# One transformer block on one core: two exponentials as powers on GpSimd, two stores issued later, a new order of the last steps, and where VectorE's transposes begin

## The chip, the core and the metric

The kernel runs on one core of one Trainium2 chip. Time is device time in microseconds (us), the median of several executions. A profile is one further execution, taken by the hardware profiler; its span runs from the first to the last instruction, and its own time is a little longer than the span.

The engines are named as in the profile: PE is TensorE's matmul stream, PEld its weight loads, DVE is VectorE, ACT is ScalarE, POOL is GpSimd and SP is SyncE, which issues most of the DMAs. A name such as L743 is line 743 of the kernel that was profiled; since the change adds lines, the same statement stands some lines lower in the changed kernel.

## The reference

The input `x` is 64 sequences of 32 tokens (2048 tokens) with 256 features. Three residual steps follow one another, each on a layer-normed `x`:

- cross attention with 16 heads to a context of 257 rows per sequence,
- self attention inside each sequence with 4 heads and rotary positions,
- a mixture of 8 experts, each token going to its two best ones.

The last is what the change touches. In short:

```python
scores = x @ Wr.T + br                       # 8 scores per token
w = softmax(scores)
idx = top_k(scores + biases_N, 2)            # two experts per token
val = w[idx] / w[idx].sum()                  # their weights
h = x @ Wl1[e] + bl1[e]; a, b = h[:512], h[512:]
y = (silu(a) * b) @ Wl2[e] + bl2[e]          # per expert e
out = x + sum over the two experts of val * y
```

## The kernel before

Tokens are worked in 16 tiles of 128 (`t` = 0 to 15). For each tile and each of its four sequences (`b`) a main loop emits the cross attention of that sequence. Between its matmuls it places pieces of other work: `near` is the rest of the tile just finished (output projection, self attention, routing), `far` the rest of the tile before that, `ahead` the queries of later tiles. The tuple `steps` says which of these is advanced at each of six places of a sequence, so it sets PE's order.

PE and SP run in the order in which the program is written. VectorE, ScalarE and GpSimd are ordered by a scheduler, so a change in the text can move instructions on them that it does not name. Each engine executes in order: an instruction that waits holds up all those behind it.

`route(t, xr)` transposes the normed tile, forms the 8 scores, finds the two best experts, forms the weights (the exponential on ScalarE at L509, then a mask, a sum, a reciprocal and a product on VectorE), counts places by a matmul (`pk`), and writes each row to its two slots of `routed` in DRAM by two indirect DMAs on GpSimd (L533). The last tiles, 14 and 15, are routed in the tail, beside expert blocks, whose Silu needs another table on ScalarE than the exponential.

The residual `x` of each tile is stored into `out` (L472) at the end of `self_attention`: from SP for tiles 0 to 13, from GpSimd's queue for 14 and 15. The experts' results are added onto `out` by scatters with an adding DMA (L743), also on GpSimd's queue.

The experts' work is cut into blocks of 128 rows of one expert. Six `early` blocks use only rows that the first tiles have routed and run beside the tail of tiles 14 and 15. When all is counted, `late_blocks` computes on VectorE a table of which expert, which rows and which weights each `late` block uses; 28 late blocks follow. A block is: `gathered` (SP loads its rows from `routed`), `prepared` (transpose to features by rows), `first_half` and `second_half` (16 matmuls each, `pa` and `pb`, with Silu on ScalarE and a product on VectorE), `combined` (8 matmuls `py`, bias, weight, scatter). Three pairs of buffers, the lanes, hold weights; block b uses lane (b + 2) % 3. A lane's weights, 1028 KB and 640 KB, are loaded only when the lane's next block has another expert, by `weights`, after the block three before has released them.

There are two ways to transpose a block. With `b < quarters`, the rows come as one DMA of 132.5 KB, PE transposes them (`pxT`, L670) and ScalarE copies the result from PSUM. Otherwise the rows come as four DMAs of 32 KB in runs of 64 floats and one of 4.5 KB, and VectorE transposes 32x32 pieces (L675). Early blocks use the first way, late ones the first for b < 3.

SP's DMAs take eight completion semaphores in turn; a DMA waits until the one eight places before it has landed. `gathered` of late block b is issued three blocks ahead. In the function `run`, for late block 0 it was issued after `last_early`, which closes the last early block and loads the weights of late block 2.

The string given to `do` writes out the tail: `near` and `far` are steps of tiles 15 and 14, `xN`, `aN`, `bN`, `cN` are prepared, first half, second half and combined of early block N.

Of the kernel before, what the change touches and what calls it, by code (L numbers as in the profile page):

```python
# [9 lines left out]
FP = mybir.dt.float32  # L10
U32 = mybir.dt.uint32
AF = mybir.ActivationFunctionType
# [4 lines left out]
P = 128  # L17
# [12 lines left out]
NE = 8  # L30
# [20 lines left out]
def block_kernel(  # L51
# [33 lines left out]
    make_identity(nc, ident)  # L85
    minus_half = const.tile([P, 1], FP, name="minus_half")
    nc.gpsimd.memset(minus_half, -0.5)
    zero = const.tile([P, 1], FP, name="zero")
    nc.gpsimd.memset(zero, 0.0)
    expert_id = const.tile([P, NE], FP, name="expert_id")  # L90
# [295 lines left out]
    def self_attention(t, xn):  # L386
# [80 lines left out]
        for k in range(2):  # L467
            nc.tensor.matmul(po, oT[:, k, :], awo_sb[:, k, :], start=(k == 0), stop=(k == 1))  # L468
        nc.vector.tensor_tensor(xs[t], po, xb, ALU.add)

        queue = nc.sync if t < NT - 2 else nc.gpsimd
        queue.dma_start(out=out[t * P : (t + 1) * P, :], in_=xs[t])  # L472

    def route(t, xr):

        nc.gpsimd.tensor_copy(xr[:, RW - 1 : RW], token[:, t : t + 1])
        xT = wk.tile([P, 2, P], FP, tag="xrT", name=f"xrT{t}")
        transposed(xT, xr, 2, f"r{t}", t < NT - 2)
        yield
        pr = bank([NE], f"pr{t}")  # L480
        for k in range(2):
            nc.tensor.matmul(pr, xT[:, k, :], wr_sb[:, k, :], start=(k == 0), stop=(k == 1))
        sc = sm.tile([P, NE], FP, tag="rsc", name=f"rsc{t}")
        nc.vector.tensor_tensor(sc, pr, br_bc, ALU.add)
        sel = sm.tile([P, NE], FP, tag="rsel", name=f"rsel{t}")
        nc.vector.tensor_tensor(sel, sc, bn_bc, ALU.add)
        top = sm.tile([P, 8], FP, tag="rtop", name=f"rtop{t}")
        nc.vector.max(top, sel)
        idx = sm.tile([P, 8], U32, tag="ridx", name=f"ridx{t}")
        nc.vector.max_index(idx, top, sel)  # L490
        idf = sm.tile([P, 2, 1], FP, tag="ridf", name=f"ridf{t}")
        nc.vector.tensor_copy(idf[:, :, 0], idx[:, 0:2])

        two = sm.tile([P, 2, NE], FP, tag="rtwo", name=f"rtwo{t}")
        nc.vector.tensor_tensor(
            two, expert_id2, idf.to_broadcast([P, 2, NE]), ALU.is_equal
        )
        both = sm.tile([P, NE], FP, tag="rboth", name=f"rboth{t}")
        nc.vector.tensor_tensor(both, two[:, 0, :], two[:, 1, :], ALU.add)
        boths[t] = both  # L500
        if t < NT - 2:


            fed = sm.tile([P, NE], FP, tag="rfed", name=f"rfed{t}")
            nc.vector.scalar_tensor_tensor(fed, both, not_last, carried[t], ALU.mult, ALU.add)
        nmx = sm.tile([P, 1], FP, tag="rnmx", name=f"rnmx{t}")
        nc.vector.tensor_reduce(nmx, sc, AX.X, ALU.max, negate=True)
        ex = sm.tile([P, NE], FP, tag="rex", name=f"rex{t}")
        nc.scalar.activation(ex, sc, AF.Exp, bias=nmx)  # L509
        nc.vector.tensor_tensor(ex, ex, both, ALU.mult)  # L510
        tot = sm.tile([P, 1], FP, tag="rtot", name=f"rtot{t}")
        nc.vector.tensor_reduce(tot, ex, AX.X, ALU.add)
        inv = sm.tile([P, 1], FP, tag="rinv", name=f"rinv{t}")
        nc.vector.reciprocal(inv, tot)
        ew = xr[:, D : D + NE]
        nc.vector.tensor_scalar(ew, ex, inv, None, ALU.mult)
        yield

        pk = bank([NE], f"pk{t}")
        if t < NT - 2:  # L520
            nc.tensor.matmul(pk, before_all, fed, start=True, stop=True)
        else:
            nc.tensor.matmul(pk, before, both, start=True, stop=False)
            nc.tensor.matmul(pk, of_last, seen[t - 1], start=False, stop=True)
        at = sm.tile([P, 1, NE], FP, tag="rat", name=f"rat{t}")
        nc.vector.tensor_tensor(at[:, 0, :], pk, region[:, 0, :], ALU.add)
        nc.vector.tensor_tensor(two, two, at.to_broadcast([P, 2, NE]), ALU.mult)
        slot = sm.tile([P, 2], FP, tag="rslot", name=f"rslot{t}")
        nc.vector.tensor_reduce(slot, two, AX.X, ALU.add)
        slots = sm.tile([P, 2], U32, tag="rslots", name=f"rslots{t}")  # L530
        nc.vector.tensor_copy(slots, slot)
        for k in range(2):
            nc.gpsimd.indirect_dma_start(  # L533
                out=routed[:, :],
                out_offset=bass.IndirectOffsetOnAxis(ap=slots[:, k : k + 1], axis=0),
                in_=xr,
                in_offset=None,
            )
        if t < NT - 1:
            seen[t] = sm.tile([P, NE], FP, tag="seen", name=f"seen{t}")  # L540
            nc.vector.tensor_tensor(seen[t], pk, both, ALU.add)  # L541
            carry(t)
# [236 lines left out]

    def late_blocks(done):  # L780

        bl = Blocks("late", LATE, lambda b: (b + 2) % LANES, 3)
        count = counted("late", NT - 2, NT - 1)
        nb = in_blocks(count, P - 1, "late")
        nc.vector.tensor_tensor(nb, nb, done, ALU.subtract)
# [65 lines left out]
    def rotary_tables():  # L851
# [78 lines left out]
        ("ahead", "far", "ahead", "near", "far", "ahead"),  # L930
        ("", "", "near", "near", "", "far"),
    )
    kvs, probs = {0: context0}, {}
    seqs = [(t, b) for t in range(NT) for b in range(4)]
    work = {"near": last_rows(), "far": iter(()), "ahead": cross_queries(0)}
# [88 lines left out]
    for n, (t, b) in enumerate(seqs):  # L1024
# [12 lines left out]
        if b == 0:  # L1037
# [4 lines left out]
            if t % 2 == 0 and t + 4 < NT:  # L1042
                for j in (t + 4, t + 5):
                    load_tokens(j)
        place = iter(steps[4 * (t % 2) + b])

        def step():
            name = next(place)
# [50 lines left out]
    def do(units):  # L1099
        for unit in units.split():  # L1100
            if unit in work:
                next(work[unit], None)
            else:
                b = int(unit[1:])
                {
                    "x": blocks.prepared,
                    "a": blocks.first_half,
                    "b": blocks.second_half,
                    "c": blocks.combined,
                }[unit[0]](b)  # L1110
                if unit[0] == "c" and b + 2 < EARLY:
                    blocks.weights(b + 2, (0, 1))

    do("near far x0")
    blocks.gathered(EARLY - 1)
    do("far near near a0 far x1 b0 near far near near c0 near a1 near far b1 x2 far a2 near c1")
    do("far near x3 b2 a3 near c2 near x4 b3 near a4")
    late, total = late_blocks(done)
    do("c3")
    for b in range(3):  # L1120
# [8 lines left out]

    def run(lo, hi, before=None):  # L1130
        for b in range(lo, hi):
            if b + 3 < hi and not (before and b == lo):
                blocks.gathered(b + 3)
            if b + 1 < hi:
                blocks.prepared(b + 1)
            blocks.first_half(b)
            if b > lo:
                blocks.combined(b - 1)
                if b - 1 + LANES < hi:
                    blocks.weights(b - 1 + LANES, (1,))  # L1140
            elif before:
                before()
                blocks.gathered(b + 3)
            blocks.second_half(b)
            if b + LANES < hi:
                blocks.weights(b + LANES, (0,))
            if b == 4:
                yield
        blocks.combined(hi - 1)
# [85 lines left out]
```

## Time and profile before

| | |
|---|---|
| median of 5 runs | 806.33 us (802.53 to 808.06) |
| the profiled execution | 807.24 us, span 805.5 us |
| PE busy | 770.8 us, 96% of the span |
| VectorE busy | 503.9 us, 63% |
| ScalarE busy | 368.9 us, 46% |
| GpSimd busy | 148.5 us, 18% |
| mean clock granted to TensorE | 0.994 |

The span has three stretches. Up to some 575 us the main loop keeps PE busy. From there to 638 us the tail of tiles 14 and 15 runs beside the six early blocks. Then come the late blocks: block 0 starts at 638.59 us; from block 6 on, at 676.03 us, they follow at 5.30 us each with no gap until 791 us; a last scatter ends the program.

In a timeline line, the columns are start, duration, engine, source line, operation, result and inputs, shape, and in brackets the idle time of the engine just before with what ended it. Where several instructions are merged, the duration is that of the group.

### The profile page before, as it was taken

The page shows a single profiled execution, that of the slowest core. Times are in us where ns is not written, and L with a number is a line of the kernel's source. Part 1 is how long each engine was busy: PE and PEld are TensorE (multiplying, and loading weights), DVE is VectorE, ACT ScalarE, POOL GpSimd, SP SyncE. Part 2 cuts the span into 40 slices and gives each one's busy share as a digit, 9 for nine tenths or more (in the row PEclk, how much of TensorE's full clock was granted, in tenths as well). Part 3 has the DMA queues.
Part 4 walks back from the last instruction along what each step waited for, and adds up shares of the span by engine and source line. Part 5 has one row for each costly group of instructions (what it writes and reads, how often), then busy time and mean ns, then how long its engine had stood idle before and what let it go on. Part 6 is the DMA issues. An engine that isn't in the chain of part 4 may idle for free.

```text
span 805.5 us, 15343 instructions
## 1 busy us (share of the span) xinstructions
PE 770.8 (96%) x5136; PEld 603.5 (75%) x5136; DVE 503.9 (63%) x2087; ACT 368.9 (46%) x1053; POOL 148.5 (18%) x211
## 2 busy tenths in 40 slices
PE   8899999999999999999999999999998989999994
PEld 7576777677767777777767777666688878999994
DVE  4657666766685677668577766768655633444442
ACT  3564556556465454546555555555426312122220
POOL 3001011120211111021111111121133312332332
PEclk9999999999999999999999999999999999999998
DMA  8540202021120202022020202110531597449432
GB/s 304 145 112 2 66 11 68 11 90 46 32 80 11 68 10 80 10 76 73 19 66 12 66 11 67 29 58 15 186 141 34 144 298 206 60 86 264 58 48 27
DMA packets 47138, 64.17 MB, mean 80 GB/s; under 512 B 22928, under 2 KB 38032, under 8 KB 45520
## 3 DMA queue, kind: packets, MB, share of 16 engines
q1 hardware_dynamic: 40528, 54.08, 21.5%
q0 software_dynamic: 6528, 9.06, 6.5%
q8 instruction: 43, 0.70, 0.4%
q14 instruction: 39, 0.32, 0.1%
HBM read 87.54 MB, written 13.16 MB: 125 GB/s over the span
## 4 chain that ended last, share of the span: by engine, by line
PE 79%; DVE 4%; DMA 3%; ACT 2%; issue 1%; POOL 1%; SPq 1%; POOLq 0%; ACTq 0%; DVEq 0%
PE pa L346 13%; PE s L313 12%; PE tp L336 7%; PE po L379 6%; PE pa_late L703 6%; PE pqh L289 5%; PE pb_late L703 5%; PE py_late L736 5%; PE pqkv L394 5%; PE pov L362 4%; PE pq L268 3%; PE apo L468 1%; ACT ov L370 1%; DMA lane<-in_wall 1%; PE pot L454 1%; DMA lane2a<-in_wall 1%
## 5 line engine op out<-in xcount | busy, mean ns | idle before, releaser
L318 ACT ACTIVATE pr<-s,nmx 128x257 f32<-128x257 f32 x256 | 122.2, 481 | 111.9 <-DVE nmx L317 100.4
L317 DVE TENSOR_REDUCE nmx<-s 128x1 f32<-128x257 f32 x256 | 105.5, 420 | 70.8 <-PE s L313 70.2
L313 PE MATMUL s<-kv,q 128*128 128x257 f32 x512 | 142.4, 387 | 1.9 <-ACT pr L318 1.4
L346 PE MATMUL pa<-pt,kv 128*128 128x512 f32 x256 | 123.3, 604 | 5.1 <-ACT ov L370 5.1
L313 PEld LDWEIGHTS s<-kv,q 128*128 128x128 f32 x512 | 89.2, 192 | 16.4 <-issue 2.7
L336 PEld LDWEIGHTS tp<-ident,pr 128*128 128x128 f32 x512 | 61.8, 144 | 30.8 <-issue 15.7
L325 DVE TENSOR_SCALAR pr<-pr,inv 128x256 f32<-128x256 f32 x256 | 80.2, 356 | 3.3
L336 PE MATMUL tp<-ident,pr 128*128 128x128 f32 x512 | 80.5, 279 | 1.6 <-DVE pr L325 1.6
L349 ACT COPY cT<-pa 128x512 f32<-128x512 f32 x64 | 37.5, 587 | 92.3 <-PE pa L346 92.3
L340 ACT COPY pt<-tp 128x512 f32<-128x512 f32 x128 | 75.5, 591 | 4.2 <-PE tp L336 3.2
L346 PEld LDWEIGHTS pa<-pt,kv 128*128 128x128 f32 x256 | 46.1, 190 | 39.6 <-issue 26.4
L743 POOL DMA_INDIRECT out_x<-y_late,to_late x28 | 43.5, 1555 | 109.8 <-DMA out_x<-y_late,to_late 41.8
L289 PE MATMUL pqh<-xqT,xwq_sb 128*128 128x256 f32 x256 | 60.8, 381 | 0.8 <-ACT xqT L196 0.8
L379 PE MATMUL po<-xwo_sb,ov 128*128 128x256 f32 x256 | 60.3, 379 | 0.0
L719 ACT ACTIVATE sa_late<-pa_late,lane 128x128 f32<-128x128 f32 x72 | 20.6, 368 | 75.0 <-PE pa_late L703 75.0
L379 PEld LDWEIGHTS po<-xwo_sb,ov 128*128 128x128 f32 x256 | 48.6, 190 | 6.6
L289 PEld LDWEIGHTS pqh<-xqT,xwq_sb 128*128 128x128 f32 x256 | 47.3, 190 | 7.9 <-ACT xqT L196 1.5
L318 ACT ACTIVATION_READ_ACCUMULATOR pr<-s,nmx 128x1 f32 x256 | 52.0, 203 | 0.0
L323 DVE RECIPROCAL inv<-sums 128x2 f32<-128x2 f32 x128 | 20.8, 162 | 46.2 <-ACT pr L318 45.5
L546 POOL TENSOR_SCALAR carried<-seen,is_last 128x8 f32<-128x8 f32 x15 | 5.3, 354 | 218.7 <-DVE seen L541 218.7
L533 POOL DMA_INDIRECT routed<-xr,rslots x32 | 33.2, 1039 | 59.6 <-DMA routed<-xr,rslots 18.3
L394 PE MATMUL pqkv<-awqkv_sb,xaT 128*128 128x512 f32 (+1 forms) x128 | 43.9, 486 | 0.0
(273 smaller groups left out, 1266.5 us busy)
## 6 DMA issues: line engine op xcount, KB each, us to landing
lane<-in_wall SPq DMA_DIRECT2D x24, 1028.0 KB
lane<-in_wall SPq DMA_DIRECT2D x24, 640.0 KB
lane2a<-in_wall SPq DMA_DIRECT2D x10, 1028.0 KB
kv<-in_ctx_t SPq DMA_DIRECT2D x16, 514.0 KB
kv<-in_ctx_a SPq DMA_DIRECT2D x16, 512.0 KB
lane2b<-in_wall SPq DMA_DIRECT2D x10, 640.0 KB
xg_late<-routed SPq DMA_DIRECT2D x100, 32.0 KB
x<-in_x SPq DMA_DIRECT2D x16, 128.0 KB
```

Of the source, the lines that this page charges most:

```text
L289: nc.tensor.matmul(pq[:, mm, :], xwq_sb[:, k, m * P : (m + 1) * P], xqT[:, k, :], start=(k == 0), stop=(k == 1),)
L313: nc.tensor.matmul(s, qb[:, g * P : (g + 1) * P], kvT[:, b, :], start=True, stop=True)
L317: nc.vector.tensor_reduce(nmx, s, AX.X, ALU.max, negate=True)
L318: nc.scalar.activation(pr[:, g, :], s, AF.Exp, bias=nmx, accum_out=sums[:, g : g + 1])
L325: nc.vector.tensor_scalar(pr[:, i, :ML], pr[:, i, :ML], inv[:, i : i + 1], None, ALU.mult)
L336: nc.tensor.transpose(tp[:, g * P : (g + 1) * P], pr[:, g, j * P : (j + 1) * P], ident)
L340: nc.scalar.copy(pt, tp)
L346: nc.tensor.matmul(pa, kvA[:, b, j, :], pts[j], start=(j == 0), stop=(j == MC - 1))
L379: nc.tensor.matmul(po, ov[:, m, :], xwo_sb[:, m, :], start=False, stop=(m == XH // 2 - 1))
L394: nc.tensor.matmul(pq, xaT[:, k, :], awqkv_sb[:, k, lo:hi], start=(k == 0), stop=(k == 1))
L703: nc.tensor.matmul(self.ps[b][half][:, j, :].rearrange("p (c i) -> p c i", c=4), w[:, lo : lo + P], self.xTs[b][:, :, k, :], start=(k == 0 ...
L743: nc.gpsimd.indirect_dma_start(out=out[:, :], out_offset=bass.IndirectOffsetOnAxis(ap=self.to[:, b : b + 1], axis=0), in_=y, in_offset=Non ...
```

## The change

Six edits.

1. A constant tile `euler` of 128x8, filled with e.
2. In `route`, for tiles 14 and 15 the exponential on ScalarE is replaced by an addition on VectorE and a power on GpSimd (e to the shifted score).
3. The stores of tiles 14 and 15 are written after the two scatters of `route` instead of at the end of self attention.
4. `late_blocks` passes 8 instead of 3 as `quarters`: late blocks 3 to 7 take the one-DMA gather and PE's transpose, and VectorE's begin with the ninth late block.
5. The last tile gets its own third row of steps, and the string of `do` is reordered: early block 0 is prepared first, and block 2 earlier.
6. In `run`, late block 3 is gathered before `last_early` instead of after it.

```diff
+    euler = const.tile([P, NE], FP, name="euler")
+    nc.gpsimd.memset(euler, math.e)
...
-        queue = nc.sync if t < NT - 2 else nc.gpsimd
-        queue.dma_start(out=out[t * P : (t + 1) * P, :], in_=xs[t])
+        if t < NT - 2:
+            nc.sync.dma_start(out=out[t * P : (t + 1) * P, :], in_=xs[t])
...
-        nc.scalar.activation(ex, sc, AF.Exp, bias=nmx)
+        if t < NT - 2:
+            nc.scalar.activation(ex, sc, AF.Exp, bias=nmx)
+        else:
+            nc.vector.tensor_scalar(ex, sc, nmx, None, ALU.add)
+            nc.gpsimd.tensor_tensor(ex, euler, ex, ALU.pow)
...
+        if t >= NT - 2:
+            nc.gpsimd.dma_start(out=out[t * P : (t + 1) * P, :], in_=xs[t])
...
-        bl = Blocks("late", LATE, lambda b: (b + 2) % LANES, 3)
+        bl = Blocks("late", LATE, lambda b: (b + 2) % LANES, 8)
...
+    last_steps = steps[4:6] + (
+        ("", "", "far", "near", "", "far"),
         ("", "", "near", "near", "", "far"),
     )
...
-        place = iter(steps[4 * (t % 2) + b])
+        place = iter(steps[4 * (t % 2) + b] if t < NT - 1 else last_steps[b])
...
-    do("near far x0")
+    do("x0")
     blocks.gathered(EARLY - 1)
-    do("far near near a0 far x1 b0 near far near near c0 near a1 near far b1 x2 far a2 near c1")
-    do("far near x3 b2 a3 near c2 near x4 b3 near a4")
+    do("near far near far near a0 far x1 b0 near far near near x2 c0 near a1 near far b1 far a2")
+    do("near c1 far near x3 b2 a3 near c2 near x4 b3 near a4")
...
-            if b + 3 < hi and not (before and b == lo):
+            if b + 3 < hi:
                 blocks.gathered(b + 3)
...
             elif before:
                 before()
-                blocks.gathered(b + 3)
```

In the built program the scheduler places the two stores a little before where the text has them. GpSimd's order in the tail, before and after (each row one instruction, k0 and k1 being the two scatters of a tile):

```
before: rstds15, store 14, rstdr14, token15, y0, y1, carried15, routed14 k0, store 15, rstdr15, routed14 k1, y2, routed15 k0, k1, y3
after:  rstds15, rstdr14, token15, y0, pow 14, y1, carried15, routed14 k0, rstdr15, store 14, routed14 k1, y2, pow 15, store 15, routed15 k0, k1, y3
```

On ScalarE the four table loads around the two exponentials are gone (Exp and Silu, twice). On PE, `trr13` moves behind a transpose and a score matmul, `pr13` behind two matmuls `pa`, `pxT` of early block 0 ahead of `pov15`, the matmuls `pss14` into the middle of `po15`, `pxT` of early block 2 ahead of `py` of block 0; five pairs of `pxT` are added for late blocks 3 to 7. On SP, 20 DMAs of the late gathers go (five gathers of one DMA instead of five).

More of the change, by code (lines that the diff above doesn't have):

```diff
@@ L932, in block_kernel @@
     )
+    last_steps = steps[4:6] + (
+        ("", "", "far", "near", "", "far"),
+        ("", "", "near", "near", "", "far"),
+    )
     kvs, probs = {0: context0}, {}
```

## The prediction

> **What bounds the kernel now.** I read the page first (shares of the span, chain), then PE's timeline from 570 us on, then what ended PE's idle times, and last the queues that those lead to: the DMA view, GpSimd, ScalarE. PE is busy for 96% of the span, so an edit gains only where PE idles or by less PE work. The chain of work that ended last leaves PE for long in the late blocks only; its window from 575 us has:
>
> ```profile
> 649.61 1.79 PE pa_late L703 x16
> 651.39 1.73 PE py_late L736 x8
> 653.12 1.77 PE pb_late L703 x16
> 654.89 8.56 DMA lane<-in_wall
> ...
> 667.72 8.18 DMA lane2a<-in_wall
> 675.89 0.14 issue
> 676.03 2.02 PE pa_late L703 x16
> ```
>
> Two weight loads of 1028 KB take over 8 us to land, and PE's timeline shows what that costs (start, duration, in brackets the idle time before):
>
> ```profile
> 638.59 1.95 PE L703 MATMUL pa_late<-bxT_late,lane2a 128*128 128x128 f32 x16
> ...
> 655.76 2.05 PE L703 MATMUL pa_late<-bxT_late,lane2a 128*128 128x128 f32 x16 [0.85 <-DVE gates_late L680]
> ...
> 663.59 2.02 PE L703 MATMUL pa_late<-bxT_late,lane 128*128 128x128 f32 x16 [2.27 <-DMA lane<-in_wall]
> ...
> 676.03 2.02 PE L703 MATMUL pa_late<-bxT_late,lane2a 128*128 128x128 f32 x16 [1.17 <-DMA lane2a<-in_wall]
> ```
>
> Blocks 0 to 6 start at 638.59, 644.12, 649.45, 655.76, 663.59, 669.32 and 676.03; block 7 follows after 5.37 and all later ones after 5.30. So 37.44 us went where 6 x 5.30 = 31.80 would do: **5.64 us**, 0.23 of them PE's own transposes. The DMA view of 640 to 676 us says why:
>
> ```profile
> DMA packets 5748, 11.06 MB, mean 307 GB/s; under 512 B 3772, under 2 KB 4287, under 8 KB 4987
> q1 hardware_dynamic: 5164, 10.48, 86.6%
> q0 software_dynamic: 580, 0.53, 11.6%
> ```
>
> The 16 engines are full (98%), two thirds of the packets being small. SP queues behind them: the ring of eight semaphores makes the small gathers wait for weights,
>
> ```profile
> SPq L643 <- DMA lane<-in_wall: 4.5, 4, 1.7
> ```
>
> In the tail, PE idles for 0.90 (573.55), 0.56, 0.44, 0.45, 0.48 us and then here:
>
> ```profile
> 613.37 1.13 PE L468 MATMUL apo<-awo_sb,oT 128*128 128x256 f32 x4 [0.66 <-DVE seen L541]
> ...
> 619.69 0.41 PE L195 MATMUL trr<-ident,xr 128*128 128x128 f32 x2 [1.39 <-DVE xr L184]
> ```
>
> For the second, GpSimd's timeline: the rstdr that `xr` needs stands behind a store that waits for a scatter to land.
>
> ```profile
> 613.50 1.58 POOL L743 DMA_INDIRECT out_x<-y_early,to_early  x1 [9.18 <-DVE rex L510]
> 614.53 0.90 POOL L546 TENSOR_SCALAR carried<-seen,is_last 128x8 f32<-128x8 f32 x1
> 615.62 1.06 POOL L533 DMA_INDIRECT routed<-xr,rslots  x1 [0.18 <-POOL carried L546]
> 617.87 0.61 POOL L472 DMA_DIRECT2D out_x<-x  x1 [1.20 <-DMA out_x<-y_early,to_early]
> 618.51 0.59 POOL L181 TENSOR_TENSOR rstdr<-ver,minus_half 128x1 f32<-128x1 f32 x1
> ```
>
> **Part by part.** I sum against the profiled execution, 807.24 us (span 805.5 and 1.7 around it); it lies 0.9 above the median of the runs, 806.33.
>
> *Steps of tiles 13 to 15.* A transpose and a score matmul (0.87 us) go ahead of `trr13`, so its 0.90 wait is covered: -0.87. `pxT` of block 0 (0.23) fills the wait for ScalarE's copy of `cT` (0.56): its own 0.23 is saved later. `pss14` behind half of `po15` covers the 0.44 wait. That makes -1.54 by `trs15`, but no more: rstds15 stands on GpSimd behind routed13 k1 (591.35, which waits for k0 to land, 6.7 us beside weight loads that don't move) and axb15 (0.74), so it starts near 593.0 as now, xns15 ends near 594.1, and `trs15` (now 595.69) can't come before 594.15. `pss14` comes no earlier, and VectorE puts `x15` (0.42) ahead of the four diagonal transposes, so `pot14` comes near 591.4, 0.1 behind PE. `pxT` of block 2 earlier removes the waits of 0.45 and 0.48, but `pot15` hangs on qkv, softmax and transposes, which keep their length, so PE waits there instead: 0. Bounds of this part: 0 (rstds15 later by as much) to -2.3 (0.87 + 0.56 + 0.44 + 0.45).
>
> *ScalarE without the exponentials.* Four table loads of 1.28 go (5.1 us of ScalarE). One lies on the path: oT15's copy, wanted from pot's end at 610.45, comes at 612.97 behind a load (611.47) and the exponential. Without them it follows the Silu that ends at 611.45, is done by 611.8, and `apo15` follows `pk14`: -0.66. The other three loads are hidden by PE work; if that were gone, the cost would be 1.28 each. The skill's page "ScalarE: Activation LUTs" (What ACT_TABLE_LOAD costs) adds a drain of about 1.38 us to each switch; here a load at 609.78 of 1.28 is followed by its Silu at 611.08, so no drain shows. By the page four switches would free 10.6 us of ScalarE, and the path would still gain the 0.66 that PE waited.
>
> *Store behind rstdr15.* rstdr15 goes ahead of the store and starts when routed14 k0 is issued, at 616.68 instead of 618.51: -1.8, of which PE's arrival leaves -1.2. `trr15` thus comes by 1.54 + 0.66 + 1.2 = 3.4 earlier. The stores move ahead of routed14 k1 and routed15 k0; each waits for a scatter's landing (3.79) and holds what is behind it. Store 15 would start some 4.3 after y2's start; routed15's second scatter then lands about 2.4 before the first late gather wants its rows (in the trace the margin is 2.1): hidden, and past that margin every us is lost.
>
> *The powers.* No row has a power of 8 columns. One column takes 0.55 (rstd); an addition of 256 columns 0.73; ScalarE's exponential 0.30. Below, the power costs what one column does, 0.55; above, eight times that, 4.4. I take **1.5**: about 0.2 fixed (from the addition) and 0.16 per column, nearer to the one-column row, because that row must hold the fixed part. What waits: VectorE's product with the mask stands right behind, then y1 and y2's bias, g, the places and `count_late`. Power 14 starts near 610.4; the product could start at 611.1 and comes at 612.0; y1's addition (now 612.41) slips by 0.4 and so do y1's scatter and rstdr15 behind it: +0.35. Power 15 stands behind y2's scatter (1.63): the product comes 1.3 later than the one of now, and the four g (4 x 0.26), which are done before it now, come after: `count_late` +1.5. Per further us of the power, each of the two adds about 1. At 0.55 the two add 0 and 0.7, at 4.4 some 3.3 and 4.4. The late table, SP's first gather and so late block 0 hang on `count_late` (the 8 us chain from 626.92 to 634.77, then 638.59): late block 0 comes by 3.4 - 0.35 - 1.5 = **1.55 earlier**, at 637.0.
>
> The page "GPSIMD Engine Reference" (4.1 Engine selection) speaks against this edit: elementwise work belongs on VectorE, being about twice as slow on GpSimd for two inputs. At its 2.6 cycles an element, eight columns would cost as good as nothing above one, and the sum would be -6.4 in place of mine; it says nothing on powers.
>
> *Late blocks 3 to 7.* PE gets 5 x 2 transposes, 0.23 a block: +1.15; ScalarE 5 copies of 0.37 and VectorE 5 transposes of 0.43 less, both hidden. The DMAs: 576 to 582 us, nearly weights alone, gives 2.58 us of the 16 engines per MB (2.42 MB at 103.9% of 6 us). In 640 to 676 the 10.48 MB hold about 0.68 of late gathers; 9.8 MB of weights take 25.2 of q1's 31.2 us, so 6.0 for five gathers, **1.2 each**. The one-DMA gathers: 0.31 MB took 42.2% of 635.1 to 638.2, 1.3 for three, so about **0.5 each**. Per block the engines now need 4.4 (weights, 1.71 MB) + 1.2 + 0.84 (a scatter, from q0) = 6.4 against PE's 5.30; after, 5.75 against 5.53. From the issue of block 1's weights (638.17) to the landing of block 6's first layer there are 9.59 MB of weights (24.7), four gathers (2.0), six scatters (5.0) and 1.6 to start (a gather's 2.17 in the chain less its 0.5): 33.3. Block 6 wants them 33.6 after that issue, 0.42 + 6 x 5.30 + 6 x 0.23. So the waits nearly go; I keep 0.5. Late: 33.2 + 0.5 from block 0 to block 6, against 37.44: **-3.75**. The gather of block 3 ahead of `last_early` is one DMA of 0.33 on SP ahead of block 2's weights, wanted 11 us later: 0. With three DMAs a block, the ring reaches 2.7 blocks back, so SP issues the weights when their lane is free. What is late next is block 6's first layer. Bounds: 0 (the DMAs still set the pace) to -4.25. From block 8 on all is as now.
>
> *The rest.* `euler` is 0.1 us beside the first loads: 0.
>
> Sum: -1.55 - 3.75 = **-5.3**: 801.9 against 807.24, **801.0** beside the median. What tells this kernel from no change is about 0.5%, 4.0 us.
>
> **Rivals.**
> A. *The powers are dear* (4.4 each, eight times the one-column row). For: one column costs three quarters of 256 additions. Against: some of the 0.55 must be fixed. Late block 0 comes 4.3 later instead of 1.55 earlier (3.4 - 3.3 - 4.4), and with -3.75 the sum is +0.55: 807.8 on the profiled scale, 806.9 beside the median, slower than before. It decides from a power of about 4.1 on.
> B. *The DMAs stay the bound.* For: 5.75 against 5.53 leaves nothing for hiccups. Against: SP's waits on the ring go. The late gain falls to between 0 and 2; at 0.5 the sum is -2.0: 804.3.
> C. *The tail gains nothing*: -1.55 is lost to GpSimd's landings, with the late gain: 802.6.
> D. *The powers are as cheap as one column, and no wait is left*: -2.7 - 4.25 = -7.0: 799.4.
>
> **How the numbers follow.** Chances: forecast 0.38, D 0.15, C 0.15, B 0.16, A 0.11, else 0.05. Range: D less 1.4 of scatter between executions gives 798; A and 0.6 of the same give 807.5. The likeliest one's own range is 799.5 to 802.5. Faster by over 0.5% (under 802.3): the forecast nearly whole, D, and some third of C and the rest: 0.59. Within 0.5%: B, the rest of C, most of A: 0.32. Slower by over 0.5% (over 810.4): a part of A and what I don't see, such as routed15 landing past its margin: 0.09.
>
> **What would show it.** Right: no table load at the two routings; the GpSimd power near 1.5; the waits of 0.66 and most of 1.39 gone; late block 0 near 637; 33 to 34 us from it to block 6; q1's packets in that stretch down by over 2,000; SP no longer waiting at a gather for weights. Wrong: a power above 3, PE idle before `pxT` of late block 0 for over 2, or weight loads still landing after 8 us.

## The result, and the profile after

The kernel after takes 803.29 us in the median of 44 runs (800.59 to 810.74); the kernel before takes 805.39 beside it (86 runs, 802.30 to 811.51). The ratio is 0.9981, with a 95% interval of 0.9970 to 0.9991: **1.5 us faster (0.7 to 2.4), where 5.3 were forecast.** That is less than the half per cent at which I would call a kernel faster. The profiled execution of after takes 803.73 us (span 802.0), that of before 807.24 (span 805.5).

The difference of 3.5 us between the two profiles can't be taken at its face. Some 2.4 us of it lie ahead of everything that the change does on the path. The stretches from 20 to 40 us of before (first fence) and of after (second) differ in one column: the one behind the engines' busy times is the granted clock of TensorE.

```profile
20.00:40.00 20.00, 17.52 (x103) 11.64 (x102) 13.53 (x45) 10.50 (x30) 1.73 (x3) 0.91 0.52 148
```

```profile
20.00:40.00 20.00, 17.59 (x109) 11.62 (x108) 12.24 (x42) 11.61 (x33) 1.78 (x3) 1.00 0.60 163
```

The clock was 0.91 there in the execution of before and 1.00 in that of after. A later execution of before's code without one scatter (e4) has 1.00 too, so it is no property of the kernel. By an estimate, 0.09 of 20 us, the clock accounts for at most 1.8 of the 2.4 us. The whole of it is there early: an earlier tile's token column is copied at 108.49 in before and at 106.08 in after, and from then on the two executions run in step until the routings change. So I count both from one mark ahead of them, GpSimd's copy of tile 13's token column into `xr`, which starts at 572.90 in before and at 570.49 in after:

```profile
570.49 0.18 POOL L477 COPY xr<-token 128x1 f32<-128x1 f32 x1
```

| us behind the mark | before | after | moved | forecast |
|---|---|---|---|---|
| `trs15` | 22.79 | 22.03 | -0.76 | -1.54 |
| `apo15` | 40.47 | 39.04 | -1.43 | -2.20 |
| `trr15` | 46.79 | 44.62 | -2.17 | -3.40 |
| `count_late` (VectorE) | 54.02 | 53.61 | -0.41 | -1.55 |
| first `pa_late` of late block 0 | 65.69 | 65.34 | -0.35 | -1.55 |
| first `pa_late` of late block 6 | 103.13 | 99.04 | -4.09 | -5.30 |
| last product scaled (VectorE) | 223.31 | 219.23 | -4.08 | -5.30 |
| last scatter issued (GpSimd) | 223.80 | 222.71 | **-1.09** | -5.30 |
| end of the span | 232.60 | 231.51 | **-1.09** | -5.30 |

PE is 4.1 us ahead when it ends. Three of them are lost between the last product and its scatter. The late blocks did what was forecast. PE's timeline of after for blocks 0, 1, 3, 4 and 6 (start, duration, in brackets the idle time before):

```profile
635.83 1.95 PE L712 MATMUL pa_late<-bxT_late,lane2a 128*128 128x128 f32 x16
641.79 2.02 PE L712 MATMUL pa_late<-bxT_late,lane 128*128 128x128 f32 x16 [0.27 <-DMA lane<-in_wall]
...
652.93 1.95 PE L712 MATMUL pa_late<-bxT_late,lane2a 128*128 128x128 f32 x16
658.47 1.95 PE L712 MATMUL pa_late<-bxT_late,lane 128*128 128x128 f32 x16
...
669.53 1.95 PE L712 MATMUL pa_late<-bxT_late,lane2a 128*128 128x128 f32 x16
```

From block 0 to block 6 PE takes 33.70 us instead of 37.44. The waits of 2.27 and 1.17 for weights are gone, and SyncE's gathers no longer wait for weights. The DMA view of 640 to 676 us has fewer packets (4577 instead of 5748), and q1's share falls. Its packets fall by 1,401 (from 5164), fewer than the 2,000 that the prediction named as a sign:

```profile
DMA packets 4577, 10.96 MB, mean 304 GB/s; under 512 B 1799, under 2 KB 3162, under 8 KB 3930
q1 hardware_dynamic: 3763, 10.18, 73.5%
```

The chain that ended last tells what sets the end now. Its last pieces in after are four scatters, one behind the other; in before only the very last one (792.21) stood there.

```profile
774.88 3.85 DMA out_x<-y_late,to_late
779.48 3.81 DMA out_x<-y_late,to_late
784.04 3.78 DMA out_x<-y_late,to_late
788.58 3.87 DMA out_x<-y_late,to_late
```

GpSimd's and VectorE's timeline of after at the end:

```profile
785.01 0.35 DVE L751 TENSOR_SCALAR y_late<-y_late,gate_late 128x256 f32<-128x256 f32 x1
...
788.58 1.55 POOL L752 DMA_INDIRECT out_x<-y_late,to_late  x1 [2.98 <-DMA out_x<-y_late,to_late]
...
789.29 0.43 DVE L751 TENSOR_SCALAR y_late<-y_late,gate_late 128x256 f32<-128x256 f32 x1
793.20 1.55 POOL L752 DMA_INDIRECT out_x<-y_late,to_late  x1 [3.07 <-DMA out_x<-y_late,to_late]
```

The same of before:

```profile
795.86 0.35 DVE L742 TENSOR_SCALAR y_late<-y_late,gate_late 128x256 f32<-128x256 f32 x1
796.70 1.55 POOL L743 DMA_INDIRECT out_x<-y_late,to_late  x1 [2.94 <-DVE y_late L742]
```

The last product is ready at 789.72 in after, and its scatter starts at 793.20, 3.48 us later, because the scatter ahead of it has to land first. In before the product is ready at 796.21 and its scatter starts 0.49 later. Every scatter adds to rows of the same `out`, and in these traces none starts before the one ahead of it has landed. At the end of after, where no weights stream, a scatter lands 3.8 to 3.9 us after its start, and the next starts 0.75 later: 4.6 in all, 1.55 of them GpSimd's own.

I call this the **scatter queue**, and the time between a product and its scatter its lag. It is seen over all 28 late blocks. Both kernels' queues lag from the first late block on, and the lags grow where expert weights stream:

| late block | 0 | 1 | 2 | 3 | 6 | 12 | 15 | 18 | 21 | 24 | 27 |
|---|---|---|---|---|---|---|---|---|---|---|---|
| lag in before | 3.5 | 5.0 | 7.4 | 9.0 | 6.3 | 3.3 | 7.7 | 5.3 | 3.2 | 1.1 | 0.5 |
| lag in after | 6.1 | 9.4 | 10.8 | 9.9 | 7.0 | 3.5 | 8.7 | 8.4 | 6.7 | 4.6 | 3.5 |

While weights stream a scatter comes only every 6 to 10 us. GpSimd's timeline of before has it in plain sight:

```profile
659.02 1.55 POOL L743 DMA_INDIRECT out_x<-y_late,to_late  x1 [5.30 <-DMA out_x<-y_late,to_late]
667.79 1.55 POOL L743 DMA_INDIRECT out_x<-y_late,to_late  x1 [7.21 <-DMA out_x<-y_late,to_late]
677.36 1.55 POOL L743 DMA_INDIRECT out_x<-y_late,to_late  x1 [8.02 <-DMA out_x<-y_late,to_late]
681.92 1.55 POOL L743 DMA_INDIRECT out_x<-y_late,to_late  x1 [3.00 <-issue]
```

Later PE needs 5.30 us for a block and the queue 4.6, so the queue catches up by 0.7 a block. In the profile of before it had just caught up when the last block came. So PE could come earlier by next to nothing before the queue set the end, unless the queue came earlier too.

### The profile page after: what moved, and what is told of

It is laid out like the page before. It is cut to its first block, busy times and chain, and to the rows that moved or that the text cites. A ratio compares the mean times of both kernels' runs of the same rounds, so it can differ in the third digit from the quotient of the medians.

```text
span 802.0 us, 15293 instructions
## 1 busy us (share of the span) xinstructions
PE 769.4 (96%) x5146; PEld 602.6 (75%) x5146; DVE 502.2 (63%) x2084; ACT 365.0 (46%) x1052; POOL 152.5 (19%) x214
## 4 chain that ended last, share of the span: by engine, by line
PE 78%; DVE 4%; DMA 3%; issue 2%; ACT 2%; POOL 1%; SPq 0%; POOLq 0%; ACTq 0%
PE pa L348 12%; PE s L315 12%; PE tp L338 7%; PE po L381 6%; PE pa_late L712 6%; PE py_late L745 5%; PE pqh L291 5%; PE pb_late L712 5%; PE pqkv L396 5%; PE pov L364 3%; PE pq L270 3%; DMA out_x<-y_late,to_late 2%; PE apo L470 1%; ACT ov L372 1%; PE pot L456 1%
```

## The experiments

Queue theory: the scatter queue sets the end of after, and hides most of what PE gained. PE theory: the last product sets the end, and what is missing is chance variation between executions. All times stand beside runs of before on the same chip; e1 to e4, e5 to e8 and e9 to e12 shared a chip each. The marks are those of the table above.

### The late blocks alone

```diff
-        bl = Blocks("late", LATE, lambda b: (b + 2) % LANES, 3)
+        bl = Blocks("late", LATE, lambda b: (b + 2) % LANES, 8)
...
-            if b + 3 < hi and not (before and b == lo):
+            if b + 3 < hi:
...
-                blocks.gathered(b + 3)
```

> The kernel before with the second part alone: eight whole-row gathers, and the gathers ahead of the weights in the order of after. Queue theory (the late scatters into out are one queue on GpSimd, each waits until the one ahead has landed, and this queue sets the end): PE goes from late block 0 to block 6 in about 33.7 us (37.4 before), so its last product comes some 3.7 us earlier, but the queue from the last early scatter to the last late one needs the 150.3 us that it took in after (643 to 793), against 153.3 in before; the last scatter starts 2 to 3.5 us after its product is ready (0.5 in before) and the time falls by 2 to 3.2 us against before, most or all of what the whole change gives. PE theory (the last product sets the end, and the missing gain is scatter between executions): the last scatter starts within 0.6 us of its product, and the time falls by 3.7 us.

Measured: 803.28 us against 804.92, ratio 0.9974 (0.9958 to 0.9990), -2.1 us. PE takes 33.32 from block 0 to block 6, and the last product comes 219.05 behind the mark, 4.3 earlier than in before. The last scatter follows at 219.82, 0.8 after its product: neither theory's lag. In the profiled execution the whole gain of PE arrives (span end 228.5 behind the mark, 232.6 before), and the queue from the last early scatter to the last late one took 149.4. So the late part can give its 4 us; in the median it gives 2.1, which can't be told from the 1.5 of the whole change.

### The tail alone

```diff
-        bl = Blocks("late", LATE, lambda b: (b + 2) % LANES, 8)
+        bl = Blocks("late", LATE, lambda b: (b + 2) % LANES, 3)
...
-            if b + 3 < hi:
+            if b + 3 < hi and not (before and b == lo):
...
+                blocks.gathered(b + 3)
```

> The kernel after with the late blocks as before (three whole-row gathers, old order of gathers and weights): powers, stores behind the scatters and the new steps alone. Queue theory: the last early scatter gains nothing (in after it starts 0.44 us earlier, in a profile whose main loop is 2.4 us ahead), so the time stays within 1 us of before, or is up to 2 us above it. PE theory: what PE gains ahead of the late blocks arrives at the end, -0.4 us (what after shows at late block 0) to -1.6 us (what was forecast).

Measured: 804.78 against 804.92, ratio 0.9991 (0.9971 to 1.0011): nothing. Late block 0 starts 65.43 behind the mark (-0.26), but the last early scatter comes at 72.03, 1.5 us *later* than in before, and at the end the queue lags by 1.9: the span ends 233.7 behind the mark. The last early scatter's product is ready at 69.96 (70.22 in before), but the scatter ahead of it had not landed: 8.2 us lie between their starts. In after it is the same (8.6 us), while in before the last early scatter waits only for its product. Why the one ahead lands later there was not shown. PE's small gain doesn't arrive, as the queue theory has it; the interval holds the small gain of the PE theory as well.

### One scatter left out, in after and in before

```diff
+            if self.name == "late" and b == 20:
+                return
             nc.gpsimd.indirect_dma_start(
```

> The kernel after without the scatter of late block 20 (its 128 rows are not added to out; all else is computed). Queue theory: the queue is 4.6 us shorter from there on, catches up with its products, and the end comes as much earlier as the last scatter lagged, 3.48 us less a last lag of some 0.3: 3.0 to 3.4 us below after (about 799.5 to 800.5 profiled if the main loop takes as long as in the profile of after). PE theory: nothing moves, within 0.3 us of after.

> The kernel before without the scatter of late block 20 (its 128 rows are not added to out). Queue theory: the queue had just caught up with PE at the end of before (the last scatter 0.49 us after its product, block 26's 0.28), so 0 to -0.4 us. PE theory: within 0.3 us of before. It is run for the difference to the same edit of after: queue theory makes the two kernels differ by 5 to 7 us once the scatter is out, against 1.5 to 3.5 with it.

Measured: after without it 801.24, ratio 0.9946 (0.9928 to 0.9965); before without it 804.89, ratio 0.9992 (0.9977 to 1.0006). So one scatter of 28 is worth 2.8 us in after (against its own ratio of 0.9981) and 0.6 in before, where the interval holds nothing as well: near the queue theory's numbers for the times (3.0 to 3.4, and up to 0.4). The two kernels then differ by 3.7 us, less than the 5 to 7 that I had expected. In the profile of e4 the last scatter of before's code comes 1.35 us after its product although one scatter is gone, so the queue binds there too in some executions. The one profile of e3 does not show it: its last lag is 4.0, because that execution's scatters were slower while weights streamed (7.7, 7.1, 8.5 us where after has 6.3, 8.4, 6.3), so the end lies 231.3 behind the mark, as in after. One profile shows only one course of the queue; this called for an experiment in which the queue can't bind at all (e9 and e10).

### After once more

> The kernel after unchanged, beside the next three on one chip. Queue theory: the last scatter starts 2 us or more after its product (3.48 in the first profile), the last early scatter stands 72 to 72.6 us behind the copy of tile 13's token column (70.5 in before and in the kernel with the late part alone, which both keep the old tail), and the time is 1 to 2.5 us below before, no lower than the late part alone (-2.1). PE theory: the first profile was a chance; the last scatter starts within 0.6 us of its product and the time is 4 to 5 us below before.

Measured: 803.66 against 805.41, ratio 0.9981 (0.9958 to 1.0005), as before; the fastest was 800.26 and the slowest 808.56. The profile fell on the fastest. PE's marks are those of the first one to 0.1 us up to the counts (`trs15` 22.04, `apo15` 39.04, `trr15` 44.62, `count_late` 53.62), and the last product comes at 218.93 against 219.23. But the queue was faster, 146.8 us instead of 150.3 from the last early scatter to the last late one, and the last lag is 0.5:

```profile
788.91 0.35 DVE L751 TENSOR_SCALAR y_late<-y_late,gate_late 128x256 f32<-128x256 f32 x1
...
789.73 1.55 POOL L752 DMA_INDIRECT out_x<-y_late,to_late  x1 [2.91 <-DVE y_late L751]
```

Its end lies 228.2 behind the mark, 3.3 earlier than in the first profile of the same kernel. So the lag of 2 us that I expected in every execution was wrong; PE's marks are the same in both profiled executions, the queue's are not. That the last early scatter stands at 72.6 was right.

### Whole-row gathers in the second stream too

```diff
-            if b < self.quarters:
+            if b < 8 or 13 <= b < 21 or self.name == "early":
```

(at both places that ask it)

> The kernel after with whole-row gathers (and TensorE transposes) for late blocks 13 to 20 as well, which are gathered while the second set of expert weights streams. Queue theory: PE pays 0.23 us in each of the eight blocks, 1.8 us in all, and that is hidden under the last lag of 3.5; the stream has some 5.6 DMA-us less in it (eight gathers of 1.2 become 0.5), the scatters' intervals there (6.3, 8.4, 6.3, 4.5, 6.4 in after) lose 1 to 3 us, and the time falls by 0.5 to 1.8 us against after. PE theory: the time rises by 1.8 us against after.

Measured: 804.02 against 805.41, ratio 0.9977 (0.9964 to 0.9990): the same as after. The last product comes 1.3 us later (220.55 behind the mark), and the time doesn't rise visibly, though intervals of 2 us and more could hide 1.3. But the queue was not faster: its intervals in the second stream are 8.3 and 10.0 instead of 6.3, 8.4, 6.3, 4.5, 6.4. Perhaps the stream is shorter with fewer gathers in it and holds the scatters up more while it lasts; that was not shown. The expected gain was wrong.

### The old order of the steps

```diff
-        place = iter(steps[4 * (t % 2) + b] if t < NT - 1 else last_steps[b])
+        place = iter(steps[4 * (t % 2) + b])
...
-    do("x0")
+    do("near far x0")
...
-    do("near far near far near a0 far x1 b0 near far near near x2 c0 near a1 near far b1 far a2")
-    do("near c1 far near x3 b2 a3 near c2 near x4 b3 near a4")
+    do("far near near a0 far x1 b0 near far near near c0 near a1 near far b1 x2 far a2 near c1")
+    do("far near x3 b2 a3 near c2 near x4 b3 near a4")
```

> The kernel after with the old order of tail steps (last tile's steps and early blocks' units as in before); powers, stores and late blocks as in after. Steps theory (the prediction: the order is worth 1.5 us to PE): late block 0 starts 0.5 to 1.5 us later than in after (65.3 us behind the copy of tile 13's token column). Queue theory: the last early scatter goes back towards 70.5 us behind that mark, because the early products come at their old distance, and the time is within 0.7 us of after or below it, although PE has less of a start. PE theory: the time rises by as much as late block 0 is later.

Measured: 805.36 against 805.41, ratio 0.9999 (0.9980 to 1.0019). `trs15` goes back to 22.79, `trr15` to 45.31, late block 0 to 66.09 (after: 22.03, 44.62, 65.34): the order is worth 0.75 us to PE, all along. The last early scatter did not go back to 70.5; it stands at 72.68, so the steps are not what delayed it. The time's interval is too wide to tell 0.75 from nothing.

### The exponentials back on ScalarE

```diff
-        if t < NT - 2:
-            nc.scalar.activation(ex, sc, AF.Exp, bias=nmx)
-        else:
-
-            nc.vector.tensor_scalar(ex, sc, nmx, None, ALU.add)
-            nc.gpsimd.tensor_tensor(ex, euler, ex, ALU.pow)
+        nc.scalar.activation(ex, sc, AF.Exp, bias=nmx)
```

> The kernel after with the last two routings' exponentials on ScalarE as in before. Powers theory (the prediction: power 14 costs 0.35, power 15 1.5 us up to the late counts; in after the products with rex waited 1.05 and 2.40 us for GpSimd): the late counts come 1 to 1.5 us earlier against tile 15's routing transposes (6.77 us behind them in after). Table theory (the loads are what the powers save): the four loads of 1.28 us come back, tile 15's output projection is 0.66 us later again, and the counts gain less than 0.5 us in all. Queue theory for the time: either way within 1 us of after, since the last scatter lags by 3.5 us; late block 0 moves by less than 1 us.

Measured: **801.68 against 805.41, ratio 0.9958 (0.9937 to 0.9979): 3.4 us below before**, the fastest of all kernels here that compute everything. What the powers cost stands in the timelines. After (GpSimd and VectorE, then the product that waits for the power):

```profile
607.24 1.68 POOL L515 TENSOR_TENSOR rex<-euler,rex 128x8 f32<-128x8 f32 x1 [5.62 <-DVE rex L514]
...
618.49 1.63 POOL L752 DMA_INDIRECT out_x<-y_early,to_early  x1 [1.52 <-DVE rtop L489]
619.51 2.33 POOL L515 TENSOR_TENSOR rex<-euler,rex 128x8 f32<-128x8 f32 x1
...
621.87 0.17 DVE L516 TENSOR_TENSOR rex<-rex,rboth 128x8 f32<-128x8 f32 x1 [2.40 <-POOL rex L515]
```

With the exponentials on ScalarE, tile 15's stands behind a table load, and VectorE does not idle for it:

```profile
618.25 1.28 ACT L510 ACT_TABLE_LOAD   x1
619.54 0.30 ACT L510 ACTIVATE rex<-rsc,rnmx 128x8 f32<-128x8 f32 x1
...
620.23 0.16 DVE L511 TENSOR_TENSOR rex<-rex,rboth 128x8 f32<-128x8 f32 x1
```

`count_late` comes at 51.70 instead of 53.61 (-1.91), and late block 0 at 63.50 instead of 65.34 (-1.84). `apo15` stays at 39.05, so with the new order of the steps the four table loads cost PE nothing there. The last early scatter comes at 70.56 instead of 72.46: tile 15's routing scatters and, behind them, the scatter of early block 3 hang on that power too. The powers thus delay PE and the queue alike, by 1.9 us each. The median moves by 2.0 us against after on the same chip, which is not clear of the noise by itself (the two ratios' intervals overlap); the marks in the profiles carry the reading. My expectation that late block 0 would move by less than 1 us was wrong. Against `trr15` the counts come 1.66 us earlier (7.33 behind it instead of 8.99; the 6.77 of the expectation does not come out of these marks), a little more than the 1 to 1.5 of the powers theory.

In the profile of this kernel the last product is 2.4 us earlier than in the first profile of after, and the last lag is 4.1 us: there the queue takes most of that, too.

### Half of the scatters left out, in after and in before

```diff
+            if self.name == "late" and b % 2 == 0:
+                return
             nc.gpsimd.indirect_dma_start(
```

> The kernel after without the scatters of the late blocks with even numbers (their rows are not added to out; all products are computed). The queue then has two block times for each scatter and can't bind. Queue theory: the last scatter starts within 0.7 us of its product and the time is that of PE's end: 1 to 2.5 us below after, and 3.7 to 4.5 us below before without the same scatters, which is the gain of PE (its last product 4.1 us earlier in the profiles) that the queue hides otherwise. PE theory: the difference to before without the same scatters stays 1.5 to 2.1 us, as it is with all scatters.

> The kernel before without the scatters of the late blocks with even numbers. Queue theory: PE's end is the end there nearly always, so the time falls by less than 1 us against before. PE theory: the same as in after without them, 0 to 1 us.

Measured: after without them 799.57, ratio 0.9923 (0.9903 to 0.9944); before without them 804.81, ratio 0.9987 (0.9971 to 1.0002); both beside 805.97. The two differ by 5.2 us, where the complete kernels differ by 1.5. The profiles have last products 218.76 and 223.00 behind the mark, ends 226.8 and 231.0, a difference of 4.2. The last scatters of e9 (first fence) and of e10 (second) wait for their products, not for a landing:

```profile
788.91 0.35 DVE L751 TENSOR_SCALAR y_late<-y_late,gate_late 128x256 f32<-128x256 f32 x1
789.54 1.55 POOL L754 DMA_INDIRECT out_x<-y_late,to_late  x1 [8.03 <-DVE y_late L751]
```

```profile
793.86 0.35 DVE L742 TENSOR_SCALAR y_late<-y_late,gate_late 128x256 f32<-128x256 f32 x1
794.49 1.56 POOL L745 DMA_INDIRECT out_x<-y_late,to_late  x1 [8.02 <-DVE y_late L742]
```

This decides for the queue theory. Before loses 1.0 us with half of its scatters gone, after 4.7 (ratio 0.9923 against 0.9981). PE is not what moved: its last products come only 0.5 and 0.3 us earlier than in the profiles with all scatters. Of both falls some 1.0 us lies behind the start of the last scatter, from which the span goes on for 7.8 and 7.7 us instead of 8.8; that is no effect of the lag, and it cancels in the difference.

The 5.2 of the medians is a little too much. The mean granted clock of e9's six executions was 0.996 to 0.998, that of e10's twelve 0.992 to 0.997; the three and the five at 0.997 differ by 4.4 us in their medians (799.60 and 803.96), close to the profiles' 4.2. For the same reason the narrow range of e9 (799.08 to 800.90, against 800.26 to 808.56 for the twelve executions of e5) does not show that the queue alone spreads after's times: e10 ranges from 802.88 to 807.02 with a queue that can't bind.

The mean clock also says something on the queue where nothing is left out. In the profile of after PE's last matmul ends at 788.79, and the clock falls to 0.50 behind it:

```profile
796.00:800.00 4.00, 0.00 (x0) 0.00 (x0) 0.00 (x0) 0.00 (x0) 0.00 (x0) 0.50 0.11 16
```

So the longer an execution goes on behind PE, the lower its mean clock. It is 0.9940 over the twelve executions of e5 and 0.9951 over the 31 of before beside them, by an estimate (0.0011 x 802 / 0.5) some 1.8 us more at the half clock. That fits an end that stands further behind PE in after, though the mean can't tell it from a low clock earlier on.

### The weights in halves

```diff
+            parts = 1 if self.name == "early" else 2
             for i in layers:
-                nc.sync.dma_start(
-                    out=lanes[self.lane(b)][i], in_=(wall1, wall2)[i][bass.ds(e * P, P), :], **cond
-                )
+                wide = (W1LEN, W2LEN)[i] // parts
+                for c in range(parts):
+                    nc.sync.dma_start(
+                        out=lanes[self.lane(b)][i][:, c * wide : (c + 1) * wide],
+                        in_=(wall1, wall2)[i][bass.ds(e * P, P), c * wide : (c + 1) * wide],
+                        **cond,
+                    )
```

> The kernel after with the exponentials on ScalarE, and each load of a late block's expert weights as two loads of half the columns (rows of 4112 and 2560 bytes in place of 8224 and 5120). Queue theory with the row size as the cause of slow scatters (a scatter's rows wait behind one weight row at a time): the scatters' intervals while weights stream (9.5, 8.5, 8.2 and later 5.5, 6.8, 7.5 in the kernel with the exponentials on ScalarE) fall by 1 to 2 us each, the last lag of 4.1 us goes below 1 and the time falls by 1 to 3 us against that kernel. Rival, bytes as the cause (the scatters wait for the bytes of the stream, whatever their rows): the intervals stay within 0.5 us, and the time stays or rises by up to 2 us, because SyncE issues two more loads in each block.

Measured: 809.84 against 805.97, ratio 1.0050 (1.0029 to 1.0072), 7.4 us above e8 by the ratios. The scatters' intervals are 9.2, 7.8, 7.8 in the first stream (9.5, 8.5, 8.2 in e8) and 7.5, 8.2, 7.3 in the second: a row of half the size does not free the scatters by 1 to 2 us each. The rival was nearer, but not right: the three long intervals of the second stream sum to 23.0 us instead of 19.8, which is more than its 0.5 each, and the time rises by more than its 2. PE now waits in the second stream:

```profile
722.34 1.83 PE L712 MATMUL pa_late<-bxT_late,lane 128*128 128x128 f32 x14 [0.92 <-DMA lane<-in_wall]
...
730.43 1.83 PE L712 MATMUL pa_late<-bxT_late,lane 128*128 128x128 f32 x14 [1.01 <-DMA lane<-in_wall]
738.07 2.51 PE L712 MATMUL pa_late<-bxT_late,lane2a 128*128 128x128 f32 x14 [2.07 <-DMA lane2a<-in_wall]
```

Whether the weights come late because SyncE issues them later or because they now share the DMAs otherwise was not told apart.

### The stores in their old place

```diff
-        if t < NT - 2:
-            nc.sync.dma_start(out=out[t * P : (t + 1) * P, :], in_=xs[t])
+        queue = nc.sync if t < NT - 2 else nc.gpsimd
+        queue.dma_start(out=out[t * P : (t + 1) * P, :], in_=xs[t])
...
-        if t >= NT - 2:
-
-            nc.gpsimd.dma_start(out=out[t * P : (t + 1) * P, :], in_=xs[t])
```

> The kernel after with the last two stores where before has them (GpSimd, right behind the sum of the attention output). Stores theory (the prediction's terms: the store ahead of tile 15's statistics cost GpSimd 0.73 us and the statistics' result 1.2 us): tile 15's routing transposes start 0.7 to 1.3 us later than in after and late block 0 as much. Rival: GpSimd has slack there and late block 0 moves by less than 0.4 us. Queue theory for the time: within 1 us of after in both cases.

Measured: 805.33 against 805.97, ratio 0.9988 (0.9969 to 1.0007). `trr15` starts 44.71 behind the mark (after: 44.62) and late block 0 at 65.46 (65.34). By the numbers the rival holds, but it is not a clean test of the store's price: with the rest of the change in place the scheduler puts tile 15's `rstdr` (43.62) ahead of store 15 (44.52) anyway, which it didn't in before (45.61 and 44.97). The store's wait can come back only with the rest undone, and that wasn't tried. The profile of this run has the largest last lag of all: 6.1 us, and 152.4 us from the last early scatter to the last late one, with PE's end where it is in after (218.78).

## Why the prediction was wrong

**What failed is the step from PE to the end.** The prediction ends its sum with "From block 8 on all is as now" and takes PE's gain for the kernel's. PE did go on as before from block 8 on; the scatters did not keep up. No rival had this: C let GpSimd's landings take the tail's gain, but left the late blocks' gain whole. It could have been read from the profile of before: the scatters that wait 7 to 8 us, a lag of 9.0 at block 3, and of 0.3 to 0.5 only at the last two. I had read the DMAs as PE's limit and counted the scatters' share of them, 0.84 us a block, but not how long each one holds the next: 4.6 us, and up to 9.6. PE's gain is 4.1 us in the profile and 4.2 to 4.4 (e9 and e10) where the queue is out of the way. What arrives is 1.5. So of the 3.8 us that are missing from the forecast's 5.3, some 2.6 are lost behind PE; the other 1.2 were never gained by PE, and lie in the tail.

**Late blocks, -3.75: right.** Block 0 to block 6 took 33.70 us, where 33.2 and a wait of 0.5 were forecast; of the waits for weights 0.27 is left.

**The powers, 1.5 each: right in their effect on PE, low in duration.** They took 1.68 and 2.33 (the second beside a scatter that GpSimd was still issuing). Up to the counts the forecast had +0.35 and +1.5, 1.85 in all; e8 shows 1.91 for both, 0.25 of them at `trr15`. What I missed is that power 15 also delays tile 15's routing scatters, the early scatter behind them, and so the queue. The rule that elementwise work belongs on VectorE (the Trainium skill, "GPSIMD Engine Reference", 4.1 Engine selection) was not tried here: no run has these powers on VectorE, and e8 shows only that ScalarE's exponentials were the better choice. The price that I worked out from the page's cycles, as good as nothing above one column, does not hold for these powers: eight columns took 1.68 and 2.33 us, one column 0.55.

**ScalarE without the exponentials, -0.66: right on its own, gone in the sum.** The wait ahead of `apo15` is gone in after, but e8, with all four loads back, has `apo15` at the same place. So with the new order of the steps PE does not wait for the loads. With the old order (e7) the powers' kernel has `apo15` at 39.65 against before's 40.47, so there they were worth about that.

**Steps, -1.54: half.** 0.76 at `trs15`, and e7 gives it back exactly. Waits that I had moved work into came back on the way: 0.49 for `pr` and 0.24 for `cT`.

**Store behind rstdr15, -1.2:** `trr15` gains about 1.0 beyond `apo15` once the powers are out (e8: 44.37 - 39.05 against 46.79 - 40.47). That this is the store's doing was not isolated. Of the 1.39 us that PE waited for `trr15`, 0.66 is left in after, where the prediction had most of it gone.

With the powers out the tail gains 2.2 us at late block 0, where 3.4 were forecast: mostly the half of the steps that did not come. In after 1.84 of them pay for the powers, and 0.35 is left of the 1.55 forecast.

The predicted 801.0 lies below the measured 803.29, which is within the range of 798.0 to 807.5 but outside the likeliest case's own, 799.5 to 802.5; by the ratio the change is one of those within half a per cent.

What stays open is why the queue takes 146.8 us in one execution of after and 150.3 in another. The differences lie where weights stream (the intervals that end at blocks 13 to 17), and PE's marks are alike in both.

## What to carry to other kernels

A gain on the busiest engine is a gain only if whatever takes its results keeps up: ahead of summing, list for the last stage when each result is ready and when its output leaves, and see how that lag runs; a lag that reaches zero only at the last block is a second bound, as near as the first. The indirect scatters of this kernel, which all add to one tensor, ran as a serial queue whose step is a landing and the next start (4.6 us, and 6 to 10 beside streamed weights), and the DMAs' mean share did not show it. And a small elementwise operation moved to an idle engine pays its price wherever its result is waited for: here the two powers took 1.84 us of the 2.2 that the tail's other edits gave PE.

## What the runs showed of the hardware that I had not expected

- A scatter of 128 rows of 1 KB landed 3.7 to 3.9 us after its start in most cases where no expert weights streamed, and up to 8.8 us after it while they did (before's profile); neither fewer gathers in the stream (e6) nor weight rows of half the size (e11) made the scatters faster in a way that counted.
- A power of 128x8 on GpSimd took 1.68 us and, beside the issue of a scatter, 2.33; of 128x1, 0.55 to 0.59.
- TensorE's granted clock was 0.91 from 20 to 40 us in two of the fourteen profiles (before and e1) and 1.00 in the others, e4 and e10 with before's code up to the late scatters among them. The mark stands at 572.90 and 572.96 in the two, and between 570.33 and 571.39 in the others. Two single profiles can thus differ by over 2 us before any edit is reached, more than this change is worth.
